# Adding every fourth state of a selective scan to the next one by an accumulating DMA

## The chip, the cores and the metric

The program runs on one core of one Trainium2 chip. The metric is device time in microseconds (us) of the whole program, the median of several runs. Engines are called as the profile calls them: PE (TensorE, with PEld for its weight loads), DVE (VectorE), ACT (ScalarE), POOL (GpSimd) and SP (SyncE, which here only issues DMAs).

## What is computed

The input x is 16 images of 192 channels and 64 x 64 pixels, all fp32. Four layers follow one another, each of the form x = x + f(group_norm(x)): layer 0 is a small per-channel chain of tanh layers that ends in a difference of sigmoids; layer 1 is a matrix over the pixel and its four neighbours; layer 2 is a selective scan in four directions; layer 3 is a sum of depthwise convolutions, a 1x1 convolution, a batch norm over all images and a clip. The change lies in layer 2, whose core is:

```
xs = [x, x transposed, x reversed, x transposed and reversed]      # 4 directions k, length L = 4096
delta = softplus(dt_projs_weight @ dts + bias)                     # per channel d
for each position l, for each channel d and each of N = 16 states n:
    h[d, n] = exp(delta[d] * A[d, n]) * h[d, n] + delta[d] * u[d] * B[n]
    y[d]    = sum over n of h[d, n] * C[n]
y = sum of the four directions (turned back), + x * D
```

So per direction and channel 16 recurrences of length 4096 run side by side, each is multiplied by its C, and the 16 products are added up.

## The kernel before

**Layout.** Two images make a pair: 2 x 192 channels are three groups j of 128 partitions, and there are 8 pairs. For each pair `scans` does layer 2 and `layer3` follows. While `scans` of a pair runs, it also carries the *front* of the next pair: group-norm statistics, layer 0, group norm, layer 1, group norm, the projection to B, C and dt, and a splitting step, written as Python generators that emit a few instructions per `next`. The front of the first pair runs alone ahead of everything. Pairs 1 to 7 therefore carry a front in their scans, the eighth carries none. A loop on the device runs six of the pairs, two in a turn; two are written out after it.

**The scan.** A *tile* t of the scan is one group j, one direction k and one of four stretches of LC = 1024 positions: 3 x 4 x 4 = 48 tiles, in the order of `todo`. Each has N = 16 *steps*, one for each state n; step s = 16 t + n, 768 steps in all. A step consists of:

- `load_c`: SP loads one row of C, spread over 128 partitions, into a tile cb of 512 KB (4 buffers), two steps ahead;
- `decay`: ACT makes dA = exp(A * delta), two steps ahead;
- `spread`: PE spreads B over the partitions, by a matmul of two passes with `pick`, into pbt in PSUM (2 buffers), two steps ahead;
- `product`: DVE multiplies pbt by du = delta * u, in place;
- `scan`: DVE's tensor_tensor_scan makes h (7 buffers) from dA and pbt; ACT copies the last column of h into `state`; POOL multiplies h by cb, in place;
- `add_up`: PE adds h to ysum in PSUM by matmuls with the identity, LC/512 = 2 of them, each of which shows as two passes in the trace. It is emitted LATE = 3 steps after the scan. At n = 0 it opens ysum with what other directions left in X or Xt, at n = 15 it closes it, and ACT copies it to X or Xt.

Once for each tile, `step_rest` makes delta and du of the next tile: PE makes v (in the same PSUM buffer as ysum), ACT and POOL make softplus out of it (ACT: Abs, Relu, Exp, two Identity, Ln; POOL: a subtraction, two additions, and the product du). Its pieces come at n = 2 and at the steps in `when_step`.

**The order.** Within `scans` every engine keeps the order in which the program emits (class `_InOrder`, whose helper line L63 is the line of nearly all instructions in the profile). So the loop `for s in range(total)` at the end of `scans` is a schedule written out by hand. In each step it emits, in this order: `load_c(s + 2)`, other loads, `product(s)`, `scan(s)`, `decay(s + 2)`, `spread(s + 2)`, pieces of `finish` (which adds X and Xt when a group j is done), a piece of `step_rest`, pieces of the front `fr`, and `add_up`. The front's pieces are counted in units: in layer 0 a `next` counts one, in layer 1 one matmul counts 0.5, in the projection 0.36. A tile of 16 steps takes 13 units of layer 0 (none at n = 2, 4 and 6), and 15 units of the other stages (none at n = 2 and 4, two at n = 3). What the front has left after the last step is emitted behind it.

Of the kernel before, what the change touches and what calls it, by code (L numbers as in the profile page):

```python
# [14 lines left out]
ALU = mybir.AluOpType  # L15
# [24 lines left out]
ORDER = (1, 3, 0, 2)  # L40
RD = 2 * R

LATE = 3

# [44 lines left out]
def conv_preact_kernel(ctx: ExitStack, tc: tile.TileContext, a: dict):  # L91
    nc = tc.nc
    x_in = a["x"]
    out = a["out"]
# [203 lines left out]
    def image(ap):  # L298
        return ap.rearrange("p (h w) -> p h w", w=HW)
# [458 lines left out]
    def scans(i, o, st3, nxt):  # L758

        E = _Engines(tc, True)  # L760
        with ExitStack() as es:
# [24 lines left out]
            cbs, dAs, pbs, hs = {}, {}, {}, {}  # L786

            def seq(t, k, at, n):


                v = image(t) if k % 2 == 0 else columns(t)
                return v[:, at // HW : (at + n) // HW, :]
# [33 lines left out]
            def load_c(s):  # L826
                t, n = divmod(s, N)
                j, k, at, first = todo[t]
                cb = cbs[s] = cp.tile([P, LC], F32, name="cb")
                src, row = (o.c, 64 + 16 * k) if k % 2 == 0 else (o.cp, 16 * (k - 1))  # L830
                for b, rows in {
                    0: ((0, slice(0, P)),),
                    1: ((0, slice(0, 64)), (1, slice(64, P))),
                    2: ((1, slice(0, P)),),
                }[j]:
                    r = row + N * b + n
                    E.sp.dma_start(
                        out=cb[rows, :],
                        in_=src[r : r + 1, at : at + LC].to_broadcast([rows.stop - rows.start, LC]),
                    )  # L840

            def step_rest(t):

                j, k, at, first = todo[t]
                bias = dtb[:, k, j : j + 1]
                dt = dts.pop(t)
                v = py.tile([P, LC], F32, name="v", tag="ysum")
                for h in range(2):  # L850
                    rows = slice(32 * h, 32 * h + RD)
                    E.pe.matmul(
                        v[:, 512 * h : 512 * h + 512],
                        dtw[rows, k, j, :],
                        dt[rows, :],
                        start=True,
                        stop=True,
                    )
                delta = two.tile([P, LC], F32, name="delta")
                e = one.tile([P, LC], F32, name="sp_e")  # L860
                w1 = one.tile([P, LC], F32, name="sp_w")
                ln = one.tile([P, LC], F32, name="sp_l")
                E.act.activation(e, v, AF.Abs, bias=bias)
                E.act.activation(delta, v, AF.Relu, bias=bias)
                yield
                E.table(TANH, LN)
                E.act.activation(e, e, AF.Exp, scale=-1.0)
                E.act.activation(w1, e, AF.Identity, bias=one_c)
                yield
                E.act.activation(w1, w1, AF.Identity, bias=minus_c)  # L870
                yield
                E.table(LN)
                E.act.activation(ln, e, AF.Ln, bias=1.0)
                yield
                E.gps.tensor_tensor(e, e, w1, ALU.subtract)
                yield
                E.gps.tensor_tensor(ln, ln, e, ALU.add)
                yield
                E.gps.tensor_tensor(delta, delta, ln, ALU.add)
                yield  # L880
                du = two.tile([P, LC], F32, name="du")
                E.gps.tensor_tensor(image(du), image(delta), seq(xns[j], k, at, LC), ALU.mult)
                made[t] = delta, du

            when_step = (4, 5, 6, 7, 8, 10, 12)

            def decay(s):
                t, n = divmod(s, N)
# [18 lines left out]
            def product(s):  # L907
                E.dve.tensor_tensor(pbs[s], made[s // N][1], pbs[s], ALU.mult)

            def scan(s):  # L910
                t, n = divmod(s, N)
                j, k, at, first = todo[t]
                if (j, k) not in state:
                    state[j, k] = sp_.tile([P, N], F32, name="state")
                dA, pbt, cb = dAs.pop(s), pbs.pop(s), cbs.pop(s)
                back = k >= 2
                flip = slice(None, None, -1) if back else slice(None)
                h = hs[s] = hp.tile([P, LC], F32, name="h")
                v = state[j, k][:, n : n + 1]
                E.dve.tensor_tensor_scan(  # L920
                    h[:, flip], dA[:, flip], pbt[:, flip], 0.0 if first else v, ALU.mult, ALU.add
                )
                E.act.copy(v, h[:, 0:1] if back else h[:, LC - 1 : LC])
                E.gps.tensor_tensor(h, h, cb, ALU.mult)

            def add_up(s):

                t, n = divmod(s, N)
                j, k, at, first = todo[t]
                h = hs.pop(s)  # L930
                to = (Xt if k % 2 else X)[:, at : at + LC]
                if n == 0:
                    ysum[t] = py.tile([P, LC], F32, name="ysum", tag="ysum")
                    for c in range(LC // 512):
                        cs = slice(512 * c, 512 * c + 512)
                        if k == 0:
                            v = xns[j][:, at + 512 * c : at + 512 * c + 512]
                            E.pe.matmul(ysum[t][:, cs], ident, xcs[t][:, cs], start=True, stop=False)
                            E.pe.matmul(ysum[t][:, cs], skip[:, j, :], v, start=False, stop=False)
                        elif k != ORDER[0]:  # L940
                            E.pe.matmul(ysum[t][:, cs], ident, to[:, cs], start=True, stop=False)
                for c in range(LC // 512):
                    cs = slice(512 * c, 512 * c + 512)
                    E.pe.matmul(
                        ysum[t][:, cs],
                        ident,
                        h[:, cs],
                        start=(n == 0 and k == ORDER[0]),
                        stop=(n == N - 1),
                    )  # L950
                if n == N - 1:
                    E.act.copy(to, ysum[t])
# [26 lines left out]
            fr = front(*nxt, E, ps, False) if nxt is not None else iter(())  # L979
            kind = None  # L980
            fin = iter(())
            gstep = iter(())
            for s in range(total):
                t, n = divmod(s, N)
                j, k, at, first = todo[t]
                if s + 2 < total:
                    load_c(s + 2)
                if n == 2:
                    load_bp(t + 1)
                if n == 4:  # L990
                    load_dt(t + 2)
                if n == 6:
                    load_xc(t + 1)
                product(s)
                scan(s)
                if s + 2 < total:
                    decay(s + 2)
                    spread(s + 2)
                if (t + 2) % (K * NC_) == 0 and n == 14:
                    load_xn(j + 1)  # L1000
                if (t + 1) % (K * NC_) == 0 and n == 5:
                    norm_xn(j + 1)
                if n > 4:
                    next(fin, None)


                if n == 2:
                    if s >= LATE:
                        add_up(s - LATE)
                    if s >= LATE and (s - LATE + 1) % (K * NC_ * N) == 0:  # L1010
                        fin = finish(j - 1)
                    gstep = step_rest(t + 1) if t + 1 < T else iter(())
                    next(gstep, None)
                elif n in when_step:
                    next(gstep, None)
                if n == 4:
                    add_up(s - LATE - 1)
                    add_up(s - LATE)
                elif n != 2 and kind != "l0":
                    done = 0  # L1020
                    while done < (1.99 if n == 3 else 0.99) and kind != "l0":
                        kind = next(fr, 1)
                        done += kind if isinstance(kind, float) else 1
                elif n not in (2, 6):
                    kind = next(fr, None)
                if s >= LATE and n not in (2, 3, 4):
                    add_up(s - LATE)
            for s in range(total - LATE, total):
                add_up(s)
# [130 lines left out]
    with tc.tile_pool(name="fin", bufs=1) as fin, tc.tile_pool(  # L1160
# [7 lines left out]
            out=zs.rearrange("p i j s -> p i (j s)"), in_=zstat_d.rearrange("i p s -> p i s")  # L1168
# [156 lines left out]
```

## Time and profile before

| | us |
|---|---|
| median of 3 runs (29407.39 to 29428.0) | 29407.53 |
| the profiled execution | 29410.14 |
| its span, first to last instruction | 29408.3 |
| scans of one pair with a front (pair 2, first to last product) | 3132 |
| scans of the last pair, without a front | 2843 |
| mean granted clock of TensorE | 0.938 |

The page of the profile starts with the busy time of each engine, its share of the span and its number of instructions. The groups further down name an instruction by line, engine, operation and tiles (out<-in) with its shapes, and give busy time, mean duration of one in ns, and the idle time of the engine just before them with what ended most of it. "SPq" is the queue in which SP issues DMAs. The 24576 passes of `add_up` are 8 pairs x 768 steps x 4. All DMAs but 24 are issued by SP, those 24 by ACT, none by POOL.

Stretches of the span are shown as start:end, length, then busy time and number of instructions of PE, PEld, DVE, ACT and POOL, the granted clock, the share of the 16 DMA engines that is busy, and GB/s. A matmul's record overlaps the next one's, so the sum of durations is above the busy time.

### The profile page before, as it was taken

To read this page: it belongs to the slowest core of one execution; us is meant where nothing else is said; L and a number is where in the kernel's file an instruction comes from. 1 tells how busy PE (TensorE), PEld (TensorE's weight loads), DVE (VectorE), ACT (ScalarE), POOL (GpSimd) and SP (SyncE) were. 2 spreads that over 40 slices of the span, in tenths; PEclk is the share of its full clock that TensorE was granted. 3 is DMA by queue.
4 is the path that set the end of the run, shared out by engine and by line. 5 is a ranking of instruction groups with operands and counts; after the bars stand their busy time and mean duration, and the time that the engine had idled before them with its cause. 6 is when DMAs were issued, how large, how long until landed. Compare 5 with 4: busy or idle time off the path is not lost. (4 is left out here: it accounts for less than half of the span.)

```text
span 29408.3 us, 221432 instructions
## 1 busy us (share of the span) xinstructions
PE 25300.0 (86%) x63284; PEld 10582.2 (36%) x63284; DVE 24784.1 (84%) x15589; ACT 17570.8 (60%) x24622; POOL 21561.7 (73%) x9672
## 2 busy tenths in 40 slices
PE   9799987999889997999979999799988999866773
PEld 4343333444333443333424333343333444322221
DVE  1399988899788997989879998898988999889994
ACT  7377545774467744777447765477545774544442
POOL 1377876778768786778767787677876878778772
PEclk9899998999999998999989999899998999999996
DMA  4456653565446653566535665356553565445545
GB/s 99 125 174 169 173 171 113 173 172 175 136 144 174 171 171 116 172 168 175 170 116 170 171 175 174 110 174 171 171 157 127 174 170 173 126 139 152 153 147 227
DMA packets 1786888, 4643.61 MB, mean 158 GB/s; under 512 B 525816, under 2 KB 526040, under 8 KB 1768240
## 3 DMA queue, kind: packets, MB, share of 16 engines
q1 hardware_dynamic: 1782192, 4578.95, 52.9%
q10 hardware_dynamic: 3456, 50.33, 0.4%
q8 instruction: 508, 8.32, 0.1%
q14 instruction: 732, 6.00, 0.1%
HBM read 3896.19 MB, written 329.51 MB: 144 GB/s over the span
## 5 line engine op out<-in xcount | busy, mean ns | idle before, releaser
L63 POOL TENSOR_TENSOR h<-h,cb 128x1024 f32<-128x1024 f32 x6144 | 14480.2, 2366 | 5298.2 <-ACT state L63 4439.8
L63 PE MATMUL ysum<-h,ident 128*128 128x512 f32 x24576 | 11806.6, 606 | 9.8 <-POOL h L63 9.7
L63 DVE TENSOR_TENSOR_SCAN h<-dA,state,pbt 128x1024 f32<-128x1024 f32 x4608 | 10814.7, 2347 | 1151.8 <-ACT dA L63 467.9
L63 DVE TENSOR_TENSOR pbt<-du,pbt 128x1024 f32<-128x1024 f32 x6144 | 7445.8, 1212 | 831.2 <-PE pbt L63 660.0
L63 ACT ACTIVATE dA<-delta,t_alog 128x1024 f32<-128x1024 f32 x6144 | 7042.2, 1147 | 60.7 <-POOL delta L63 58.4
L63 PEld LDWEIGHTS ysum<-h,ident 128*128 128x128 f32 x24576 | 4756.4, 194 | 5473.9 <-issue 4973.2
L63 ACT COPY state<-h 128x1 f32<-128x1 f32 x6144 | 1138.2, 185 | 5504.0 <-DVE h L63 5466.1
L63 PE MATMUL pbt<-bp,pick 96*128 96x512 bf16 x8192 | 2566.9, 396 | 1541.1 <-DVE h L63 1516.4
L63 DVE TENSOR_TENSOR_SCAN h<-dA,pbt 128x1024 f32<-128x1024 f32 x1536 | 3512.4, 2287 | 384.0 <-ACT dA L63 185.5
L63 PE MATMUL p<-t,wts 96*128 96x512 f32 x5376 | 2814.1, 623 | 70.4 <-ACT t L63 70.4
L63 PE MATMUL p<-m,wms 128*96 128x512 f32 (+1 forms) x5376 | 2691.9, 602 | 11.1 <-ACT lu L63 7.3
L63 ACT ACTIVATE t<-p,bias 96x512 f32<-96x512 f32 x2688 | 1806.3, 679 | 1404.4 <-PE p L63 1398.6
L63 PEld LDWEIGHTS <-pick 96*128 96x128 bf16 x8192 | 720.0, 100 | 4283.2 <-DVE h L63 2347.1
L1087 POOL TENSOR_TENSOR l_g<-l_g,l_m 128x1024 f32<-128x1024 f32 x672 | 1614.4, 2404 | 433.1 <-ACT l_g L1083 349.0
L63 PE MATMUL l_p<-l_xp,w1s 128*128 128x512 f32 x3920 | 1881.3, 605 | 0.0
L1110 DVE SCALAR_TENSOR_TENSOR l_p<-xp,wc,l_p 128x1024 f32<-128x1024 f32 x1248 | 1589.7, 1287 | 285.6 <-PE l_p L1104 254.8
L63 PE MATMUL pbt<-bp,pick_mix 96*128 96x512 bf16 x4096 | 1262.6, 390 | 531.0 <-DVE h L63 529.0
L1092 PE MATMUL l_p<-xp,diag 128*128 128x512 f32 x2688 | 1288.7, 639 | 352.1 <-DVE l_y L1110 281.3
L63 PEld LDWEIGHTS p<-t,wts 96*128 96x128 f32 x5376 | 1046.6, 197 | 1237.0 <-issue 914.9
L63 POOL TENSOR_TENSOR sp_e<-sp_e,sp_w 128x1024 f32<-128x1024 f32 x384 | 908.5, 2366 | 529.5 <-ACT sp_l L63 356.1
L1083 ACT ACTIVATE l_m<-xp,wc 128x1024 f32<-128x1024 f32 x672 | 779.8, 1163 | 835.2 <-POOL l_g L1087 835.2
L63 PEld LDWEIGHTS p<-m,wms 128*96 128x96 f32 (+1 forms) x5376 | 949.0, 177 | 716.5 <-issue 343.7
(224 smaller groups left out, 21596.0 us busy)
## 6 DMA issues: line engine op xcount, KB each, us to landing
cb<-cp_d SPq DMA_DIRECT2D x2048, 512.0 KB
cb<-c_d SPq DMA_DIRECT2D x2048, 512.0 KB
cb<-cp_d SPq DMA_DIRECT2D x2048, 256.0 KB
cb<-c_d SPq DMA_DIRECT2D x2048, 256.0 KB
m<-l_xn SPq DMA_DIRECT2D x3072, 128.0 KB
bp<-bp_d SPq DMA_DIRECT2D x384, 192.0 KB
f0x<-in_x SPq DMA_DIRECT2D x96, 512.0 KB
l_x<-in_x SPq DMA_DIRECT2D x192, 256.0 KB
```

The source lines that it names most:

```text
L63: return self._tc.keep_in_program_order(call(*args, **kw))
L1083: nc.scalar.activation(image(m), window(j, 16 * c, 16, tap), AF.Copy, scale=factor(j, tap))
L1087: nc.gpsimd.tensor_tensor(g, g, m, ALU.add)
L1092: nc.tensor.matmul(ps[:, cs], diag[:, j, t, :], window(j, 16 * c + 8 * h, 8, tap), start=(t == 0), stop=False,)
L1110: nc.vector.scalar_tensor_tensor(image(y if tap is TAPS[-1] else ps), window(j, 16 * c, 16, tap), factor(j, tap), image(ps), ALU.mult, ALU ...
```

## The change

In `scan`, when n % 4 is 1, POOL issues, behind its multiplication of h, a DMA that adds the h of the step before (n % 4 = 0) to this h, in SBUF. That h of the step before leaves the list `hs`, and `add_up` passes it over: it adds three states of four, and opens ysum at n = 1. LATE is 4. The order written out in the loop is changed with it: `step_rest` starts at n = 3 and its pieces come at 5, 6, 7, 8, 10 and 12, with the Ln and the first subtraction in one piece; the front takes 15 units of layer 0 in 16 steps (two at n = 0 and 12, none at 3, 5 and 7) and 18 units of the other stages (two where n % 4 is 0, none at 3 and 5).

```
-LATE = 3
+LATE = 4
...
                 E.act.activation(ln, e, AF.Ln, bias=1.0)
-                yield
                 E.gps.tensor_tensor(e, e, w1, ALU.subtract)
...
-            when_step = (4, 5, 6, 7, 8, 10, 12)
+            when_step = (5, 6, 7, 8, 10, 12)
...
                 E.gps.tensor_tensor(h, h, cb, ALU.mult)
+                if n % 4 == 1:
+                    E.gps.dma_start(out=h, in_=hs.pop(s - 1), accum_op=ALU.add)
 
             def add_up(s):
 
                 t, n = divmod(s, N)
+                if s < 0 or n % 4 == 0:
+                    return
...
-                if n == 0:
+                if n == 1:
                     ysum[t] = py.tile([P, LC], F32, name="ysum", tag="ysum")
...
-                        start=(n == 0 and k == ORDER[0]),
+                        start=(n == 1 and k == ORDER[0]),
...
-                if n == 2:
-                    if s >= LATE:
-                        add_up(s - LATE)
+                if n == 3:
+                    add_up(s - LATE)
                     if s >= LATE and (s - LATE + 1) % (K * NC_ * N) == 0:
                         fin = finish(j - 1)
                     gstep = step_rest(t + 1) if t + 1 < T else iter(())
                     next(gstep, None)
                 elif n in when_step:
                     next(gstep, None)
-                if n == 4:
-                    add_up(s - LATE - 1)
-                    add_up(s - LATE)
-                elif n != 2 and kind != "l0":
+
+                if kind == "l0":
+                    for _ in range({0: 2, 3: 0, 5: 0, 7: 0, 12: 2}.get(n, 1)):
+                        kind = next(fr, None) if kind == "l0" else kind
+                elif n not in (3, 5):
                     done = 0
-                    while done < (1.99 if n == 3 else 0.99) and kind != "l0":
+                    while done < (1.99 if n % 4 == 0 else 0.99) and kind != "l0":
                         kind = next(fr, 1)
                         done += kind if isinstance(kind, float) else 1
-                elif n not in (2, 6):
-                    kind = next(fr, None)
-                if s >= LATE and n not in (2, 3, 4):
+                if n != 3:
                     add_up(s - LATE)
```

## The prediction

> **What bounds the kernel now.** I read the page's first part, then busy time by stretch: one of the seven pairs whose scans carry the next pair's front, and the last pair, which carries none.
>
> ```profile
> PE 25300.0 (86%) x63284; PEld 10582.2 (36%) x63284; DVE 24784.1 (84%) x15589; ACT 17570.8 (60%) x24622; POOL 21561.7 (73%) x9672
> ...
> 4738.00:7870.00 3132.00, 2888.72 (x7291) 1215.04 (x7292) 2824.83 (x1704) 2061.36 (x2952) 2462.60 (x1087) 0.96 0.59 172
> 25826.00:28669.00 2843.00, 2007.11 (x4967) 771.71 (x4968) 2670.82 (x1552) 1274.91 (x1861) 2259.79 (x962) 0.95 0.48 151
> ```
>
> The columns of the stretches are length, then busy time of PE, PEld, DVE, ACT and POOL, granted clock, DMA share, GB/s. Both hold the same 768 steps. With a front a step takes 3132/768 = 4.08 us and PE is the fullest engine (2889 us, 92%); without one it takes 2843/768 = 3.70 us and DVE is (2671 us, 94%). So in seven pairs PE sets the pace, and DVE stands close behind. Split by stage (l0 is layer 0's part of the front, l1 layer 1's):
>
> ```profile
> 4858.00:6757.00 1899.00, 1809.34 (x4586) 764.59 (x4587) 1718.59 (x995) 1478.83 (x2123) 1507.28 (x661) 0.97 0.61 171
> 6883.00:7489.00 606.00, 594.99 (x1528) 258.91 (x1529) 554.85 (x347) 250.65 (x366) 494.35 (x226) 0.99 0.53 168
> ```
>
> PE is busy 95% of l0 and 98% of l1, at 470 and 150 steps (multiplications by cb in these stretches), 4.04 us a step each. The timeline of TensorE inside l1 shows what a step is made of:
>
> ```profile
> 14028.36 0.60 PE L63 MATMUL pbt<-bp,pick 96*128 96x512 bf16 x2
> 14028.80 1.88 PE L63 MATMUL l_p<-l_xp,w1s 128*128 128x512 f32 x4
> 14030.51 1.88 PE L63 MATMUL ysum<-h,ident 128*128 128x512 f32 x4
> 14032.23 0.60 PE L63 MATMUL pbt<-bp,pick 96*128 96x512 bf16 x2
> ```
>
> From start to start the spread costs 0.44 us, two front matmuls (four passes) 1.71, adding one state 1.72: 3.87 us, with no gap. DVE in the last pair repeats at 3.58 us:
>
> ```profile
> 26415.44 2.35 DVE L63 TENSOR_TENSOR_SCAN h<-dA,state,pbt 128x1024 f32<-128x1024 f32 x1
> 26417.71 1.21 DVE L63 TENSOR_TENSOR pbt<-du,pbt 128x1024 f32<-128x1024 f32 x1
> 26419.02 2.35 DVE L63 TENSOR_TENSOR_SCAN h<-dA,state,pbt 128x1024 f32<-128x1024 f32 x1
> ```
>
> Last, the groups and waits around the state, which the change touches:
>
> ```profile
> L63 POOL TENSOR_TENSOR h<-h,cb 128x1024 f32<-128x1024 f32 x6144 | 14480.2, 2366 | 5298.2 <-ACT state L63 4439.8
> L63 PE MATMUL ysum<-h,ident 128*128 128x512 f32 x24576 | 11806.6, 606 | 9.8 <-POOL h L63 9.7
> ...
> L63 SPq DMA_DIRECT2D cb<-cp_d x4096: 314/444/2002, 1202.5 to 28185.4; - x196
> ...
> SPq L63 <- POOL h L63: 14222.5, 5037, 22.8
> ```
>
> POOL has idle time and PE hardly ever waits for it; SP's queue, however, lives from POOL's progress, since a cb buffer comes free when POOL has multiplied.
>
> **The change, part by part.** The profiled execution took 29410.1 us (span 29408.3), 2.6 over the shown median of 29407.5; the sum is made against 29410.
>
> 1. *Removed:* one state of four goes to ysum no more: 192 states a pair, four passes each. A pass is busy 11806.6/24576 = 0.480 us, so PE loses 192 x 4 x 0.480 = 369 us a pair: 2889 becomes 2520 with a front, 2007 becomes 1638 without. The last pair gains nothing, PE isn't its bound.
>
> 2. *What is late next:* DVE. It does the same work. The last pair lasts 172 us longer than DVE is busy; the same margin on a pair with a front gives 2825 + 172 = 2997, and that is the floor: at most 3132 - 2997 = 135 us a pair.
>
> 3. *Added on POOL:* 192 DMA issues a pair, each behind a multiplication that must have ended. No DMA is issued by POOL in this trace, so the price d is bounded: below by SP's issue of an equally large, 128-row transfer, 0.44 us (the cb row); above by POOL's costliest pass over a whole tile, 2.86 us (X<-X,Xt, mean 2856 ns in the same pair). A gain is excluded, POOL loses no work. I take 1.3: nearer to the issue row, because a list of 128 rows is made and 131,072 elements aren't touched, but well above it for the second operand and for the drain of the multiplication before it. That is 250 us a pair: POOL 2463 becomes 2713, or 90% of 2997. Behind the issue wait the next multiplication and, in steps 7 to 12 of 16, the four softplus operations; behind those SP's cb loads, ACT's dA and DVE's product of the next tile.
>
> The Trainium skill ("DMA: Bandwidth & Descriptors", Specifications) gives a first-byte latency of about 1 us for DMAs issued from GpSimd; by that, as an estimate, POOL would be at 2655 instead. No row here shows it.
>
> 4. *Added on the DMA engines:* 192 transfers of 512 KB a pair. Queue q1 moved 4579 MB in 52.9% of 16 engines' span, 18.4 GB/s an engine, so a plain 512 KB takes 1.8 us and one that reads both tiles and writes one, at most three times that, 5.3 us; shared evenly with cb loads, up to 11. I take 5 (the issue included it's 6). The DMA share of 0.59 rises by 192 x 1.8/3000 = 0.12 to, at three times that, 0.35. The lower is hidden; the upper, 0.94, would make cb late.
>
> 5. *LATE = 4:* PE wants a state after four more steps and the front's matmuls, about 4 x 3.9 + 2 = 17 us after its scan. The multiplication ends 2.7 us after the scan when POOL is free, and up to some 8 us later in the softplus steps (POOL's timeline has four multiplications in a row behind du). With 6 us for the DMA that is 9 to 17: covered, and just so in the worst steps. Uncovered, PE stalls, in order, with the next spread behind it. I put 48 us a pair on this (0.25 us a DMA; 0 to 2.5). The seven h buffers don't bind: one is wanted again seven steps later.
>
> 6. *Moved:* the front advances 15 units in 16 steps instead of 13 in l0, and 18 instead of 15 elsewhere. In l0 sixteen steps cost PE: spread 16 x 0.44, adding 12 x 1.72, v and the carry-in 3.4, waits for the copy of ysum 1.9 (371 us of PEld's waits for Xt in 192), front 15 x 1.72: 58.7, or 3.67 us a step (before: 16 states and 13 units, 62.2, 3.89, measured 4.04). So l0's measured step becomes about 3.67 x 4.04/3.89 = 3.81. In l1 adding falls by 6.9 and the front grows by 3 x 1.72 = 5.2: nearly the old step, in five sixths of the steps. The front ends some 110 steps earlier, and those run at the last pair's 3.70. Softplus begins one step later and its Ln shares a step with the first subtraction; POOL's four operations keep their steps: nothing.
>
> A rule of the skill speaks against the change. The row first: POOL's multiplications last 2327 at least, 2357 at the median and 4426 ns at most (the cb tile's rows), so something rarely holds POOL up. The skill ("SBUF — State Buffer", Who interferes with whom) says that DVE in a two-port mode locks GpSimd out and starves DMAs issued there of descriptors, and that an operation with one SBUF input outside those modes doesn't; DVE's product and scan read one full tile from SBUF and one from PSUM, so by the second half the trap is nearly shut. If each issue waited out a 2.35 us scan, 451 us more a pair, POOL would be at 3164 and the pair slower than now. The sum doesn't use this.
>
> *Sum for a pair with a front:* floor 2997 plus 48 from point 5: 3045, 87 less than 3132; seven times, -609. *Last pair:* POOL goes from 2260 to 2510 of 2843; some issues hold up the following product: +20, taken between 0 and 48. Everything outside the scans, 29410 - 7 x 3132 - 2843 = 4643 us, is untouched. 29410 - 609 + 20 = 28821, less the 2.6: **28820 us**, 2.0% faster.
>
> **The rivals.** *POOL becomes the bound (slower).* With DVE's margin of 172 us on top, a pair lasts 2463 + 192d + 172 and equals 3132 at d = 2.6 us: there it decides. At d = 2.86 it lasts 3184 (+52) and the last one 2981 (+138): 29410 + 364 + 138 = 29910. At 4 us it would be 3403 and 3200, 31660. For it: POOL is already at 79%, and its load is bunched in steps 7 to 13, with two DMAs among them. Against: its 670 us (3132 - 2463) idle a pair. 0.17.
>
> *The DMA lands late.* PE has 2997 - 2520 = 477 us to spare, 172 of it margin: 305/192 = 1.6 us a DMA are free on average, and each further one costs 192 us a pair. At 2.3 us the pair is at 2997 + 0.7 x 192 = 3131 and nothing is won; at 3 us at 3266, total 30350. The DMA share at its upper end goes with it. 0.15: 0.07 within 0.2%, 0.08 slower.
>
> *Less of the gain arrives*: d near 2, POOL at 2847 plus 172 = 3019, and stalls of the same 48 us: 3067, with 60 more in the last pair, 29410 - 455 + 60 = 29015; up to 29300. 0.17.
>
> *It does nothing:* if PE was not the bound, neither relief nor a denser front would show. The stretches speak against it: 0.01, counted with the same.
>
> **How the numbers follow.** Forecast 0.50, its own range 28465 (the floor, 29410 - 7 x 135) to 28980. A measurement of this kernel can't tell 0.2% (60 us) from no change. Faster by over that: 0.50 + 0.17 = 0.67; within: 0.07 + 0.01 = 0.08; slower: 0.17 + 0.08 = 0.25. The range goes from 28400, a little below the floor for a smaller DVE margin, to 29950, POOL at the upper bound of d.
>
> **What would show it.** Right: ysum passes 24576 to 18432; a stretch of a pair near 3045 with DVE the fullest engine at 93%, PE near 2520; issues on POOL's queue near 1.3 us; ysum's wait for the DMA under 50 us a pair; the last layer-1 matmul some 90 steps earlier. Wrong: POOL without idle time, SP waiting for it longer than 14222 us and cb late; or TensorE waiting for h's DMA by hundreds of us; or issues above 2.6 us.

## The result, and the profile after

The changed kernel takes 30150.42 us (30132.34 to 30151.98, 4 runs), the one before 29411.24 beside it: ratio 1.0249, 95% interval 1.0231 to 1.0267, so 2.5% slower where 2.0% faster was forecast, and 200 us above the range. The profiled execution's span is 30150.2 us.

The page of the changed kernel: busy time, the new DMA queue, four groups and the new issue. (Helper lines are L64 here.)

```profile
PE 24032.5 (80%) x57140; PEld 9744.0 (32%) x57140; DVE 24837.0 (82%) x15589; ACT 17541.7 (58%) x24587; POOL 22917.2 (76%) x11208
...
q0 software_dynamic: 221184, 805.40, 14.0%
...
L64 POOL TENSOR_TENSOR h<-h,cb 128x1024 f32<-128x1024 f32 x6144 | 15102.9, 2508 | 3943.0 <-ACT state L64 3627.5
L64 DVE TENSOR_TENSOR_SCAN h<-dA,state,pbt 128x1024 f32<-128x1024 f32 x4608 | 10814.4, 2347 | 1870.1 <-DMA h<-h 816.8
L64 PE MATMUL ysum<-h,ident 128*128 128x512 f32 x18432 | 9589.6, 646 | 35.8 <-DMA h<-h 35.6
...
L64 POOL DMA_DIRECT2D h<-h x1536 | 1353.8, 881 | 496.0 <-POOL h L64 396.2
...
h<-h POOLq DMA_DIRECT2D x1536, 512.0 KB, 6.9
```

The change does what it says: a quarter of ysum's passes are gone, and 1536 DMAs are issued, each for 0.88 us of POOL after 0.32 us of idleness (496.0/1536) and with 6.9 us to landing. PE lost 1268 us of busy time. But no engine gained from it: PE, DVE, ACT and POOL are all less than 83% busy, and the scan, whose duration is unchanged, now waits for "DMA h<-h".

By stretch: pair 2, its stages l0 and l1, and the last pair (length, busy PE, PEld, DVE, ACT, POOL, clock, DMA share, GB/s).

```profile
4843.00:8079.00 3236.00, 2706.73 (x6519) 1098.66 (x6520) 2838.13 (x1704) 2058.08 (x2947) 2631.41 (x1279) 0.91 0.75 198
4959.00:6705.00 1746.00, 1537.43 (x3766) 626.79 (x3765) 1510.50 (x869) 1366.82 (x1962) 1414.42 (x686) 0.95 0.76 197
6821.00:7348.00 527.00, 490.04 (x1222) 208.79 (x1223) 464.99 (x303) 206.31 (x301) 465.78 (x231) 0.96 0.78 205
26570.00:29411.00 2841.00, 1956.72 (x4196) 733.38 (x4197) 2668.57 (x1552) 1275.13 (x1861) 2427.38 (x1154) 0.81 0.68 186
```

The last pair is as long as before (2841 against 2843). A pair with a front is 104 us longer (3236 against 3132), and 7 x 104 = 728 is nearly the whole loss of 739 us. Layer 0 took 1746 us instead of 1899, but in 406 steps instead of 470: 4.30 us a step. Layer 1: 527 us in 123 steps, 4.28. After the front's end the steps take 3.65. Nothing is saturated in l0 (PE 88%, DVE 87%, POOL 81%).

Where DVE waits, an instance in l0, first on POOL, then on DVE:

```profile
5510.33 0.88 POOL L64 DMA_DIRECT2D h<-h  x1 [0.30 <-POOL h L64]
```

```profile
5512.72 2.35 DVE L64 TENSOR_TENSOR_SCAN h<-dA,state,pbt 128x1024 f32<-128x1024 f32 x1
5514.98 1.21 DVE L64 TENSOR_TENSOR pbt<-du,pbt 128x1024 f32<-128x1024 f32 x1
5518.65 2.35 DVE L64 TENSOR_TENSOR_SCAN h<-dA,state,pbt 128x1024 f32<-128x1024 f32 x1 [2.46 <-DMA h<-h]
```

This DMA landed at 5518.53, and the scan that stands idle for it starts 0.12 us later. The whole kernel has 500 such waits of DVE, 1060.6 us together. Matched by landing time, when step s issues a DMA it is the scan of s + 4 that waits for its landing in 386 of the 500, that of s + 3 in 104 and that of s + 5 in 10. That scan doesn't read anything of the DMA; it writes into the buffer that the DMA reads. The state of step s - 1 has its last reader in the DMA, which the program emits earlier than an `add_up` four steps behind, so its buffer is given back early and handed out again four to six steps after its own scan, mostly five, not seven. In l0 a landing comes some 14 us after the scan of s ends, in the median (the multiplication ends 6.4 us behind the scan, then 0.3 of idleness, then 7 from issue to landing). DVE at its own pace would start the scan of s + 4 already 4 x 3.58 - 2.26 = 12.1 us after it.

### The profile page after: what moved, and what is told of

It is laid out like the page before. It is cut to its first block, busy times and chain, and to the rows that moved or that the text cites. A ratio compares the mean times of both kernels' runs of the same rounds, so it can differ in the third digit from the quotient of the medians.

```text
span 30150.2 us, 211709 instructions
## 1 busy us (share of the span) xinstructions
PE 24032.5 (80%) x57140; PEld 9744.0 (32%) x57140; DVE 24837.0 (82%) x15589; ACT 17541.7 (58%) x24587; POOL 22917.2 (76%) x11208
## 5 line engine op out<-in xcount | busy, mean ns | idle before, releaser
L64 POOL TENSOR_TENSOR h<-h,cb 128x1024 f32<-128x1024 f32 x6144 | 15102.9, 2508 | 3943.0 <-ACT state L64 3627.5
L64 DVE TENSOR_TENSOR_SCAN h<-dA,state,pbt 128x1024 f32<-128x1024 f32 x4608 | 10814.4, 2347 | 1870.1 <-DMA h<-h 816.8
L64 PE MATMUL ysum<-h,ident 128*128 128x512 f32 x18432 | 9589.6, 646 | 35.8 <-DMA h<-h 35.6
L64 DVE TENSOR_TENSOR pbt<-du,pbt 128x1024 f32<-128x1024 f32 x6144 | 7431.9, 1210 | 454.3 <-PE pbt L64 277.3
L64 ACT ACTIVATE dA<-delta,t_alog 128x1024 f32<-128x1024 f32 x6144 | 7040.5, 1147 | 60.5 <-POOL delta L64 58.4
L64 PEld LDWEIGHTS ysum<-h,ident 128*128 128x128 f32 x18432 | 3861.1, 210 | 4406.4 <-issue 4014.8
L64 PE MATMUL pbt<-bp,pick 96*128 96x512 bf16 x8192 | 2783.6, 425 | 2956.7 <-DVE h L64 2923.0
L64 ACT COPY state<-h 128x1 f32<-128x1 f32 x6144 | 1142.9, 186 | 6678.7 <-DVE h L64 6638.3
L64 DVE TENSOR_TENSOR_SCAN h<-dA,pbt 128x1024 f32<-128x1024 f32 x1536 | 3512.6, 2287 | 605.6 <-DMA h<-h 243.8
L64 PE MATMUL p<-t,wts 96*128 96x512 f32 x5376 | 2868.2, 634 | 243.8 <-ACT t L64 243.4
L64 PE MATMUL p<-m,wms 128*96 128x512 f32 (+1 forms) x5376 | 2817.5, 629 | 46.2 <-ACT t L64 24.4
L64 PEld LDWEIGHTS <-pick 96*128 96x128 bf16 x8192 | 692.0, 102 | 5847.0 <-DVE h L64 4153.1
L64 ACT ACTIVATE t<-p,bias 96x512 f32<-96x512 f32 x2688 | 1797.5, 678 | 1052.4 <-PE p L64 1045.7
L64 PE MATMUL pbt<-bp,pick_mix 96*128 96x512 bf16 x4096 | 1314.2, 404 | 873.3 <-DVE h L64 842.2
L64 PE MATMUL l_p<-l_xp,w1s 128*128 128x512 f32 x3920 | 1923.1, 624 | 21.6 <-POOL l_xp L64 21.6
L64 POOL DMA_DIRECT2D h<-h x1536 | 1353.8, 881 | 496.0 <-POOL h L64 396.2
L64 PEld LDWEIGHTS p<-t,wts 96*128 96x128 f32 x5376 | 1047.7, 199 | 1492.9 <-issue 913.2
L64 POOL TENSOR_TENSOR sp_e<-sp_e,sp_w 128x1024 f32<-128x1024 f32 x384 | 942.7, 2455 | 722.8 <-ACT sp_l L64 477.5
```

Source lines behind the costliest of these rows:

```text
L64: return self._tc.keep_in_program_order(call(*args, **kw))
```

## The experiments

Theory A: this early reuse is the loss. Theory B: the denser front is. Theory C: POOL's issue is. "Before" was run beside each group; its medians lie between 29400 and 29411 us.

| run | what | us | ratio to before (95%) |
|---|---|---|---|
| e1_rotate | changed, buffers in strict turn | 29739 | 1.0112 (1.0095 to 1.0129) |
| e2_dropped | e1 without the DMA, a quarter of the states left out | 29269 | 0.9952 (0.9936 to 0.9969) |
| e3_order_alone | changed order, no DMA, PE adds all | 30199 | 1.0270 (1.0253 to 1.0287) |
| e4_sparse_front | changed, old rates of the front | 29973 | 1.0192 (1.0175 to 1.0209) |
| e5_rotate_sparse | e1 with old rates | 29111 | 0.9898 (0.9881 to 0.9914) |
| e6_dropped_sparse | e2 with old rates | 28682 | 0.9754 (0.9738 to 0.9770) |
| e7_late_alone | e3 with old rates | 29532 | 1.0041 (1.0027 to 1.0055) |
| e8_narrow_dma | e1, DMA of an eighth of the columns | 29731 | 1.0109 (1.0093 to 1.0126) |
| e9_shifted | e5, DMAs at n = 1, 3, 5, 15 | 29026 | 0.9868 (0.9852 to 0.9885) |
| e10_singles | e1, 15 units of layer 0 one by one | 29515 | 1.0036 (1.0022 to 1.0050) |
| e11_balanced | e5, units moved to n = 0, 4, 8, 12 | 29459 | 1.0018 (1.0009 to 1.0028) |
| e12_pool_time | e6, POOL busy as long as a DMA's issue | 29172 | 0.9920 (0.9903 to 0.9936) |

### The buffers: e1_rotate

```
-            hp = pool("l2h", 7)
+            hp = pool("l2h", 1)
-                h = hs[s] = hp.tile([P, LC], F32, name="h")
+                h = hs[s] = hp.tile([P, LC], F32, name="h", tag=f"h{s % 7}")
```

> The changed kernel with one edit: the seven h buffers are taken in strict turn (step s gets buffer s mod 7), so that the buffer which a DMA reads from is written again seven steps after its own scan instead of five. Nothing else moves. Theory A (buffer): DVE's 1061 us of waiting for the DMA of h go below 150 us, and with them the loss: 28900 to 29300 us. Theory B (density): the step is stretched by the denser front on PE, the wait moves to another place, 30050 to 30200 us. Theory C (POOL): the issue and its drain on POOL make all multiplications late, 29800 to 30200 us.

29739 us: 411 less than the change. DVE's waits before the scan (total us, times, longest), first in the changed kernel, then in e1:

```profile
DVE h L64 <- DMA h<-h: 1060.6, 500, 7.1
DVE h L64 <- ACT dA L64: 636.3, 650, 6.0
```

```profile
DVE h L64 <- ACT dA L64: 985.7, 850, 6.9
```

The wait for landings is gone, but a part of it comes back as a wait for ACT. Theory A is right about the mechanism and explains 411 us, not the whole, so its number fails; the kernel is still 1.1% slower than before.

### Without the DMA: e2_dropped

```
                 if n % 4 == 1:
-                    E.gps.dma_start(out=h, in_=hs.pop(s - 1), accum_op=ALU.add)
+                    hs.pop(s - 1)
```

> As e1_rotate, but without the DMA: the state of every fourth step is multiplied by cb and then left out of the sum, so y lacks a quarter of its states. It shows what the relief of PE is worth when neither an issue on POOL nor a transfer nor a landing is paid. Theory A: a little below e1_rotate, 28600 to 28950 us (the floor of the prediction is 28465). Theory B: 29900 us or more, since the front is as dense. Theory C: 28600 to 28950 us with e1_rotate still near 30100.

29269: the DMA costs 470 us of e1_rotate's time even with the buffers mended, and with no DMA and a quarter of PE's adding gone only 0.5% is won. None of the three theories' numbers holds: both B and C have a part.

### The order alone: e3_order_alone

```
-                if n % 4 == 1:
-                    E.gps.dma_start(out=h, in_=hs.pop(s - 1), accum_op=ALU.add)
...
-                if s < 0 or n % 4 == 0:
+                if s < 0:
...
-                if n == 1:
+                if n == 0:
...
-                        start=(n == 1 and k == ORDER[0]),
+                        start=(n == 0 and k == ORDER[0]),
```

> The changed kernel's order alone: LATE = 4, softplus one step later and the denser front, but no DMA, and PE adds all four states as before. PE has the old work in fewer steps with a front and the rest without. Theory A: PE-bound for the steps with a front, about the old time, 29300 to 29550 us. Theory B: the denser front is what costs, 29900 us or more.

30199, by itself as slow as the change. Theory A's number fails here, B's holds. PE is busy 96% of l0, at 4.25 us a step, then idles in the steps after the front:

```profile
4955.00:6684.00 1729.00, 1657.50 (x4170) 692.36 (x4169) 1487.53 (x869) 1368.90 (x1962) 1325.41 (x584) 0.98 0.60 167
7337.00:8080.00 743.00, 562.36 (x1396) 216.54 (x1395) 649.51 (x383) 380.04 (x541) 554.57 (x239) 0.95 0.50 164
```

The prediction's own sum for 16 states and 15 units, 65.6 us in 16 steps times 4.04/3.89, gives 4.26. With PE as the bound, the front must be spread evenly; the old rates ended it in step 757 of 768, the new ones in 652.

### The old rates: e4_sparse_front, e5_rotate_sparse, e6_dropped_sparse, e7_late_alone

In each the same edit, on the changed kernel, e1, e2 and e3 in turn:

```
-                    for _ in range({0: 2, 3: 0, 5: 0, 7: 0, 12: 2}.get(n, 1)):
+                    for _ in range({3: 0, 5: 0, 7: 0}.get(n, 1)):
...
-                    while done < (1.99 if n % 4 == 0 else 0.99) and kind != "l0":
+                    while done < (1.99 if n == 0 else 0.99) and kind != "l0":
```

> The changed kernel with the front's old rates, 13 units of layer 0 and 15 units of the other stages in 16 steps, all else as changed, the DMA and the early reuse of its source buffer included. Theory A: DVE still waits for landings, in more steps with a front but each less loaded: 29900 to 30300 us, with over 800 us of DVE waiting for the DMA. Theory B: the loss goes away, 29450 us or less.

> The changed kernel with both edits at once: buffers of h in strict turn, and the front at its old rates (13 and 15 units in 16 steps). Theory D (the costs add: the denser front, the early reuse of the buffer, and the DMA itself each cost what the first runs show): e4_sparse_front less the 411 us that the turn of buffers gave, 29450 to 29650 us, so still not faster than before. Rival (with both removed PE's relief shows at last): 29000 to 29300 us.

> As e5_rotate_sparse, without the DMA; the state of every fourth step is left out of the sum, so y lacks a quarter of its states. The relief of PE alone, at the old rates of the front. Theory D: 470 us (e1_rotate less e2_dropped) below e5_rotate_sparse, 28950 to 29200 us. If PE's relief is worth what the prediction took, 28465 to 28700 us.

> As e3_order_alone, with the front at its old rates: what is left of the change is LATE = 4 and softplus one step later; no DMA, PE adds all four states. It splits the 789 us that e3_order_alone cost. If the density costs them: 29350 to 29550 us. If the later adding or the later softplus does: 29850 us or more.

e4 came to 29973, inside theory A's range and 177 less than the change, with DVE waiting 1290.3 us for landings. e5 came to 29111, inside its rival's range and not theory D's, and 1.0% faster than before: the two stalls of the change had hidden each other in part. e6 to 28682, the number of "PE's relief is worth what the prediction took". e7 to 29532: adding a step later, with softplus a step later, costs 125 us by itself; the rest of e3's 789 is the density. All four pairs of runs together:

| | old rates | denser front | the density costs |
|---|---|---|---|
| no DMA, PE adds four of four | 29532 | 30199 | 667 |
| no DMA, three of four (a quarter left out) | 28682 | 29269 | 587 |
| with the DMA, buffers in turn | 29111 | 29739 | 628 |
| with the DMA, buffers as changed | 29973 | 30150 | 177 |

Read downwards, at the old rates (at the denser ones in brackets): PE's relief is worth 850 (930) us, the DMA costs 429 (470), the early reuse 862 (411).

### What of the DMA costs: e8_narrow_dma, e12_pool_time, e9_shifted

```
-                    E.gps.dma_start(out=h, in_=hs.pop(s - 1), accum_op=ALU.add)
+                    E.gps.dma_start(out=h[:, 0:128], in_=hs.pop(s - 1)[:, 0:128], accum_op=ALU.add)
```

> As e1_rotate, but the DMA adds only the first 128 of 1024 columns (512 B a row instead of 4 KB; y lacks a quarter of its states in the other columns): as many rows to issue, an eighth of the bytes. It splits the 470 us between e2_dropped (29269) and e1_rotate (29739). If POOL's time for the issue costs them: 29600 to 29750 us. If the traffic beside the cb loads or the time to landing does: 29270 to 29450 us.

29731 against e1's 29739: an eighth of the bytes, the same time. The landing comes sooner, and PE's waits for it, 94.5 us at the weight loads and 43.4 at the matmuls in e1, are no longer among the waits. So neither the traffic nor this wait costs anything that can be measured. The DMA's row in e1 and in e8:

```profile
h<-h POOLq DMA_DIRECT2D x1536, 512.0 KB, 6.8
```

```profile
h<-h POOLq DMA_DIRECT2D x1536, 64.0 KB, 4.6
```

In e12, on e6:

```
-                    hs.pop(s - 1)
+                    g = hs.pop(s - 1)[:, 0:464]
+                    E.gps.tensor_tensor(g, g, cb[:, 0:464], ALU.mult)
```

> As e6_dropped_sparse (28682), with a multiplication of 464 columns of the dropped state by cb on POOL where the DMA was issued; by the 1269 ns of a 512-column one in the profile of before it takes about 1.15 us, as long as the 0.88 us issue with the 0.30 us wait before it. y still lacks a quarter of its states. It asks what of the DMA costs 429 us (e5_rotate_sparse, 29111). If it is POOL's time: 29000 to 29200 us. If it is the landing that PE and DVE wait for: 28700 to 28850 us.

29172, 490 us more than e6, about what the DMA costs (429). So about as much time on POOL, without any DMA, costs as much, although POOL has idle time left. The stand-in isn't the same work, though: it reads two tiles from SBUF, which the issue is not shown to do. A part of the path shows in layer 0's last operation on DVE, which reads two tiles from SBUF. Its group in e6, e5 and e12:

```profile
L64 DVE SCALAR_TENSOR_TENSOR l_x<-sg,l_x 128x512 f32<-128x512 f32 x168 | 550.8, 3279 | 0.0
```

```profile
L64 DVE SCALAR_TENSOR_TENSOR l_x<-sg,l_x 128x512 f32<-128x512 f32 x168 | 724.6, 4313 | 0.0
```

```profile
L64 DVE SCALAR_TENSOR_TENSOR l_x<-sg,l_x 128x512 f32<-128x512 f32 x168 | 831.7, 4950 | 0.0
```

The same instruction takes 774 ns in the front that runs alone. In these three runs DVE stands in it the longer the busier POOL is: 174 us more in e5 than in e6, 281 more in e12. The Trainium skill ("SBUF — State Buffer", Who interferes with whom) has the rule: a VectorE instruction with two SBUF inputs contends with a GpSimd instruction that reads SBUF. The rows agree. How much of the 429 and 490 us comes this way isn't isolated.

In e9, on e5:

```
-                if n % 4 == 1:
+                if n in (1, 3, 5, 15):
...
-                if s < 0 or n % 4 == 0:
+                if s < 0 or n in (0, 2, 4, 14):
```

> As e5_rotate_sparse, but the four DMAs of a tile are issued at n = 1, 3, 5 and 15 instead of 1, 5, 9 and 13, away from the steps 7 to 13 in which POOL also does softplus (the states of n = 0, 2, 4 and 14 are added to their next ones). It asks why a DMA costs 429 us (e5_rotate_sparse less e6_dropped_sparse) although issue and drain fit into POOL's idle time. If the bunching on POOL in the softplus steps costs them: 28750 to 28950 us. If POOL's time as such does, wherever it is: 29050 to 29200 us.

29026, between the two ranges: the fastest version that adds all states, 1.3% below before. Away from softplus the l_x group falls to 528.5 us, 196 less than in e5 with as many DMAs, but only 85 us of time come back. The profiled runs show where the rest went: a pair with a front is 30 us shorter than in e5 in the mean, 7 x 30 = 210 in all and nearly half of the 66 that the DMA costs there, but the last pair is 70 longer (2807 to 2877) and the time outside the pairs some 50. So the new places have a price of their own, and the bunching, with the blocking of DVE that goes along with it, costs more than 85 us in the pairs with a front.

### What of the density costs: e10_singles, e11_balanced

```
-                    for _ in range({0: 2, 3: 0, 5: 0, 7: 0, 12: 2}.get(n, 1)):
+                    for _ in range({5: 0}.get(n, 1)):
```

> As e1_rotate (29739), with 15 units of layer 0 in 16 steps as there, but one in each step except n = 5, instead of two at n = 0 and 12 and none at 3 and 7. It asks what about the denser front costs. If it is the number of units (each unit's 1.72 us of PE no longer hides beside DVE): 29600 to 29850 us. If it is two units in direct succession, on which PE and ACT wait for one another: 29250 to 29450 us.

29515, between the two: 224 us less than e1. That this is the waiting of PE and ACT on one another isn't shown: PE's weight loads wait longer for ACT's tanh than in e1 (780.5 us against 686.8), while the l_x group falls from 718.4 to 534.2 us.

In e11, on e5:

```
-                    for _ in range({3: 0, 5: 0, 7: 0}.get(n, 1)):
+                    for _ in range({0: 2, 2: 0, 3: 0, 4: 2, 5: 0, 6: 0, 7: 0, 8: 2, 10: 0, 12: 2, 14: 0}.get(n, 1)):
...
-                elif n not in (3, 5):
+                elif n not in (2, 3, 5, 10, 14):
...
-                    while done < (1.99 if n == 0 else 0.99) and kind != "l0":
+                    while done < (1.99 if n % 4 == 0 else 0.99) and kind != "l0":
```

> As e5_rotate_sparse (29111), with the same 13 and 15 units in 16 steps, but two in each step in which PE has no state to add (n = 0, 4, 8, 12) and one in five to seven of the others. PE's work is then 3.87 us in each step that has a front. If PE's work is limited step by step, since pbt has two buffers only: 28850 to 29020 us. If the sum over many steps is what counts: 29050 to 29170 us. If double units hurt: 29250 us or more.

29459, 348 us more than e5 at equal rates: filling the steps that the change relieves is the wrong move. PE's weight loads for layer 0 then wait for ACT's tanh; first e5, then e11:

```profile
PEld p L64 <- ACT t L64: 503.0, 333, 3.5
PEld p L64 <- ACT lu L64: 58.6, 100, 1.4
```

```profile
PEld p L64 <- ACT t L64: 944.0, 680, 4.0
PEld p L64 <- ACT lu L64: 441.6, 507, 2.7
```

Two units in succession need ACT between them, and PE and ACT keep their order, so adding and spreading stand behind. Taking layer 0's units one by one removes about a third of the density's cost (224 of 628; e10 left the other stages as they were). That the rest is the number of units is only what e10 leaves; its path wasn't isolated.

## Why the prediction was wrong

*Point 1, PE's relief: right in size, in part by luck.* 850 us measured (e7 to e6), where the floor allowed 945. But 92 of them come from the last pair (2889 us in e7, 2797 in e6), which was to gain nothing. PE's busy time was mis-sized: a pass takes 9589.6/18432 = 0.520 us, not 0.480, and PE is busy 2707 us in a pair with a front, not 2520. The granted clock fell from 0.96 to 0.91 there; by its ratio alone a pass would take 0.480 x 0.96/0.91 = 0.506.

*Point 2, the floor of 2997 us:* e6's pairs take 3034, near it. Nothing with a DMA came there.

*Point 3, POOL's issue:* d is 0.88 + 0.32 = 1.20 us, 1.3 was taken. (The estimate of 2655 us beside it took a latency for time on POOL; POOL is busy 2631 us in that pair.) But that it hides, because POOL is only 90% full, failed: the DMA costs 429 us with nothing else changed (e6 to e5), and e12 shows that about as much time on POOL alone does as much. The sum had only the last pair's 20 us for it; in the profiled runs that pair pays 10 (e6 2797, e5 2807), each pair with a front 66 (3034, 3100). The starvation by DVE that was weighed against the change doesn't show in the issues: they last 867 ns at least, 878 at the median.

*Point 4, the transfer:* 6.9 us to landing instead of 6, a DMA share of 0.75, inside the bounds; free, as taken (e8).

*Point 5, "The seven h buffers don't bind: one is wanted again seven steps later":* this step failed. The buffer that the DMA reads is wanted again after five, mostly, and DVE, not PE, waits for the landing: this costs 411 us in the change, 862 at the old rates. PE's own wait for the DMA is small, 35.6 us at the matmuls and 70.2 at the weight loads in the whole kernel. The 48 us a pair were put on the wrong engine. That softplus a step later costs nothing wasn't tested by itself; together with LATE = 4 it costs 125 us (e7).

*Point 6, the denser front:* this step failed as well. It was to help, and it costs 587 to 667 us, or 177 where the early reuse stands beside it. l0 was to take 3.81 us a step; it takes 4.30, and 4.13 with neither DMA nor early reuse (e2). The sum of PE's work holds where PE is saturated (e3: 4.26 worked out, 4.25 measured). With PE relieved, no engine is full in l0 (e2: PE 91%, DVE 89%) and the step is longer than any engine's sum; that the queues then wait for one another fits e11's rows, but isn't shown as the whole cause. The 63 steps of l0 that are saved cost 3.65 us each at the end, 230 us, and l0 got shorter by only 171 (e6 1847 to e2 1676).

*The rivals:* none held. "POOL becomes the bound" had the sign but wanted d over 2.6; "the DMA lands late" had the wait but put it on PE, where 1.6 us a DMA were free. On DVE, the next bound, a landing after some 14 us is already 2 late. "It does nothing" is excluded by e6.

So the change loses by its surroundings: from 29407 the later adding costs 125, the relief gives 850, the DMA costs 429, the early reuse 862, the denser front 177 more: 30150. The shares hold for this order only; the costs of the early reuse and of the denser front hide each other in part.

## What to carry to other kernels

When a relieved engine stands just above the next one, ask of each new wait what it does to that next one: here a buffer freed by a transfer instead of a matmul was wanted two steps sooner, mostly, and stalled VectorE, which had little slack. Count when each buffer's last reader ends, not how many buffers there are. Spread the work carried along evenly over all steps, in single pieces. And an engine that is idle a fifth of the time isn't free: its instructions can slow another engine's, and they stand in the chains that other queues wait for.

## What the runs showed of the hardware

- An accumulating DMA of 512 KB from SBUF to SBUF kept the DMA engines busy for 0.140 x 16 x 30150/1536 = 44 us of one engine, against 1.8 x 16 = 29 for a plain transfer at q1's mean rate before, and landed after 6.9 us in the median.
- With less work TensorE was granted a lower clock: the mean is 0.938 to 0.942 in the kernels in which PE adds four states of four (before, e3, e7) and 0.887 to 0.907 in all that add three. In the last pair, from e7 to e6, 0.95 became 0.82 and PE's busy time fell from 2015 to 1939 us, so a quarter less adding hardly shows in busy time there.
- An accumulating DMA of 128 rows took 0.88 us of GpSimd to issue whether a row had 4 KB (e1: 881 ns in the mean) or 512 B (e8: 880).
